# A two-layer conditioned block with Strassen products: a start on quarters of Wq and Wk, three more two-level products in one layer, x^T added by GpSimd, and a rewritten output stage

## The chip, the cores and the metric

One core of a Trainium2 chip runs the whole program. The metric is the device time of one execution in microseconds (us); the kernel before takes 1194.61 us, the median of three runs (1192.78 to 1195.8).

## The reference, cut to what matters

Four batches of 512 tokens and 512 features go through two stages, all in float32. In the code V is 512, HID is 2048.

```
q, k, v  = x @ Wq, x @ Wk, x @ Wv
attn_out = softmax(q @ k^T * 512**-0.5) @ v @ Wp + bp
cms      = gelu(attn_out @ cW1 + cb1) @ cW2 + cb2 + one_hot(code)
modifier = gelu(concat(attn_out, cms) @ mW1 + mb1) @ mW2 + mb2
y        = clip(x + cms + modifier, 0, 1)
# second stage; W_down (512x256), W_up (256x512), b_*, ln_* are picked
# for each batch out of three by an index
h        = gelu(y @ W_down[e] + b_down[e]) @ W_up[e] + b_up[e] + y
out      = (h - mean(h)) * rsqrt(var(h) + 1e-5) * ln_w[e] + ln_b[e]
```

Every output of every row is computed from all of these; the large products are those with cW1, cW2, mW1 and mW2.

## The kernel before, in words

**Products.** The kernel holds activations feature-first (features on the 128 partitions, tokens along the free dimension) and works on two batches (a pair) at a time, so a block of 1024 tokens is halved into its two batches. The large products are done with the seven products of Strassen's scheme (in Winograd's form) in place of eight, numbered 1 to 7 in the code: 1 = a11 b11, 2 = a12 b21, 3 = s4 b22, 4 = a22 t4, and 5, 6, 7 = s1 t1, s2 t2, s3 t3. Sums of weights (s) are formed by GpSimd (`weight_sums`, L178 to L181), sums of activations (t) by VectorE (`token_sums`, L190). A product is called one-level when each of its blocks is multiplied plainly, and two-level when the block is once more split into seven.

**Stages, in order.** (1) The fold: Wq^T and Wk^T are turned on TensorE with a multiplication by the identity (`transposed`, L416), their blocks and sums are evacuated from PSUM (`left_from_psum`, `right_from_psum`, L681 and L641), and `folded` multiplies Wq*Wk^T in seven products of `small_product` (L659). Then x of batch 0 and 1 is turned (L416 again). (2) Attention for pair 0 and pair 1 (L595, L659). (3) For each pair four layers: `c1_layer` (cW1; one-level products at L1065, two-level at L1014), `second_layer` for cW2 (L1215), `m1_layer` for mW1 (L1131, all products two-level), `second_layer` for mW2 (L1215). (4) For each batch an adapter: `load_adapter` gathers the weights by indirect DMA (L1286), and `adapter` turns y (`res_ps`, L1314), adds b_up on GpSimd (L1318), multiplies by W_down (L1323) and W_up (L1335), adds the turned y (L1343) and normalises (L1345 to L1369). The adapters of pair 0 run inside `c1_layer` of pair 1, step by step; those of pair 1 close the kernel.

**In `c1_layer`** products 1 and 5 of cW1 are two-level (`c1_two_level`), and 2, 6, 7, 3 and 4 one-level. The order is `FIRST_C = (2, 1, 5, 6, 7, 3, 4)`. Sums of cW1 for the two-level products (`c1_inner`) are made once by GpSimd in stage 2, stored to DRAM and fetched by both pairs.

**Who orders what.** Weights come through four buffers `wslot` of 1 MB, taken in turn; their fetches stand on the SP queue (`nc.sync`), so a fetch is issued when the product that used its buffer is done. GpSimd does the expansions of weights as a list of steps (`expansion()` for cW1, cW2 and mW1 in stages 2 and 3, `late_expansion()` for mW2 beside `m1_layer` of pair 0), and its queue also issues the stores of these sums. Its instructions stand in one order with those DMAs. Some VectorE instructions are pinned in program order (`keep_in_program_order`); the rest are placed by a scheduler. PSUM has eight banks, used in turn.

**Buffers that matter below.** `slot` 0 to 7 are 1 MB buffers (`wide` is slots 0 and 1). `late_expansion` loads raw weights into slots 6 and 7, which `second_operands` of the next layer writes with VectorE (L190), pinned. `mod` is scratch in `c1_layer` and the result of mW2 after it. After `m1_layer`, two DMAs with an adding write (L1419) put x^T onto `cms`.

Of the kernel before, what the change touches and what calls it, by code (L numbers as in the profile page):

```python
# [8 lines left out]
F32 = mybir.dt.float32  # L9
# [9 lines left out]
def kernel(  # L19
# [103 lines left out]
    wq = weight((nc.sync, nc.scalar, nc.sync, nc.scalar), Wq, slot[0])  # L123
    wk = weight((nc.sync, nc.scalar, nc.sync, nc.scalar), Wk, slot[1])
# [12 lines left out]
    x_rows = [load_x(0, nc.scalar, x_places[0])]  # L137
    wv = weight((nc.scalar, nc.scalar), Wv, slot[2])
    x_rows.append(load_x(1, nc.sync, x_places[1]))
# [34 lines left out]


# [19 lines left out]
    def flat(t):  # L195
# [3 lines left out]

    c1_outer = [spill.tile([P, 3, 2, 2, 256], F32, name=f"c1_outer{u}") for u in range(2)]  # L200
    c1_inner = {
        (p, u): spill.tile([P, n], F32, name=f"c1_inner_{p}_{u}")
        for p, n in ((1, 1024), (5, 2048))
# [13 lines left out]
    def expand_c1(u, then):  # L217
# [23 lines left out]
        yield  # L241

# [43 lines left out]
    def expand(unit, raw, pairs, last, then):  # L286
# [46 lines left out]
        else:  # L333
# [3 lines left out]
            yield from plain((1, a11, two), (4, a22, one))  # L337
            yield from full((5, one), (7, three), (6, two))
            then()

    def expand_all(units, raw, pairs, last):
        if last is None:
            load_raw(*units[0][:2], units[0][3], raw)
        for n, unit in enumerate(units):

            def then():
                if n + 1 < len(units):
                    load_raw(*units[n + 1][:2], units[n + 1][3], raw)

            yield from expand(unit, raw, pairs, last, then)  # L350
# [19 lines left out]
    def late_expansion():  # L370

        yield from expand_all(m2_units, slot[6:8], (flat(mod[0]), flat(mod[1]), slot[0]), None)
# [38 lines left out]
    def transposed(get, dst, finish=None):  # L411

        ps = [bank("tr_ps") for d in range(4)]
# [5 lines left out]
        for d in range(4):  # L419
            if finish is None:  # L420
                evacuate(dst[:, d, :], ps[d])
            else:
                finish(d, ps[d])
# [228 lines left out]
    def small_product(lhs, rhs, keep, then=None, copy=nc.scalar.copy):  # L652


        def matmuls(p, _, ps, first_):
# [14 lines left out]
            (1, 5, 6, 2, 7, 3, 4), then, copy,  # L670
# [5 lines left out]
    def left_from_psum(t, s):  # L676

        s1, s2, s3, s4 = (s[:, k] for k in range(4))

        def finish(d, ps):  # L680
            nc.scalar.copy(t[:, d, :], ps)  # L681
            c = d % 2
            if d < 2:
                minus(s3[:, c], ps[:, :256], t[:, c, 256:])
            else:
                minus(s2[:, c], ps[:, 256:], s3[:, c])
                add(s1[:, c], ps[:, 256:], t[:, c, 256:])
                minus(s4[:, c], ps[:, :256], s2[:, c])

        return finish  # L690

    def folded(lhs, rhs, w, s):
# [17 lines left out]
        small_product(lhs, rhs, keep)  # L710
# [71 lines left out]
    def first_operand(pair):  # L782
        xT, t_x = places(pair)
        transposed(chunks(x_rows[2 * pair]), xT[0], right_from_psum(xT[0], sums_in(flat(t_x[0]))))
# [17 lines left out]
    transposed(chunks(wq), wq_t, left_from_psum(wq_t, s_q))  # L802
    transposed(chunks(wk), wk_t, right_from_psum(wk_t, t_k))
    lhs_qk = folded(left_operand(wq_t, s_q), right_operand(wk_t, t_k), w_qk, sums_in(slot[0]))
    first_operand(0)
    load_bias()
    begun = both_operands(0)
    for pair in range(B // 2):
# [59 lines left out]
        if pair == 0:  # L868
            begun = {}
            then = {6: [lambda: first_operand(1)], 4: [lambda: begun.update(both_operands(1))]}  # L870
# [89 lines left out]
    def c1_operands(slots=(0, 1, 2, 3)):  # L960

        at0, at1, t12, t34 = (in_rows[i] for i in slots)
        b11, b12, b21, b22 = at0[:, 0:2, :], at1[:, 0:2, :], at0[:, 2:4, :], at1[:, 2:4, :]
        t1, t2, t3, t4 = t12[:, 0:2, :], t12[:, 2:4, :], t34[:, 0:2, :], t34[:, 2:4, :]

        def inner_sums(k, t):
            s = mod[1][:, 2 * k : 2 * k + 2, :].rearrange("p a (b n) -> p (a b) n", b=2)
            return inner_operands(t, 1, [s[:, i : i + 1, :] for i in range(4)], pinned=True)
# [4 lines left out]
        one = {1: inner_sums(0, b11)}  # L973
        minus(t1, b12, b11)

        def rest():
            one[5] = inner_sums(1, t1)
# [6 lines left out]
        return one, {2: b21, 3: b22, 4: t4, 6: t2, 7: t3}, rest()  # L984
# [531 lines left out]
```

## Time and profile before

| | us |
|---|---|
| three runs: median (lowest to highest) | 1194.61 (1192.78 to 1195.8) |
| the profiled execution, its device time | 1194.26 |
| its span, first to last instruction | 1192.5 |
| TensorE (matmul) busy | 1168.9 |
| VectorE / ScalarE / GpSimd busy | 883.5 / 294.9 / 482.7 |
| TensorE's first instruction, last end | 4.39, about 1181.1 |

The device time is 1.76 us above the span, and the profiled execution is 0.35 us below the median. A float32 matmul stands in the trace as two passes, each with a weight load (PEld); a turn by the identity is one pass. "128x512" is partitions by elements. In the views, the number in brackets is the idle time of the engine ahead of the line, with what ended it. The duration of one matmul (379 or 592 ns) includes its latency; what a pass costs in a row of matmuls is read from the distance of their starts. Idle time of TensorE sums to 23.6 us (1192.5 - 1168.9).

### The profile page before, as it was taken

The page shows a single profiled execution, that of the slowest core. Times are in us where ns is not written, and L with a number is a line of the kernel's source. Part 1 is how long each engine was busy: PE and PEld are TensorE (multiplying, and loading weights), DVE is VectorE, ACT ScalarE, POOL GpSimd, SP SyncE. Part 2 cuts the span into 40 slices and gives each one's busy share as a digit, 9 for nine tenths or more (in the row PEclk, how much of TensorE's full clock was granted, in tenths as well). Part 3 has the DMA queues.
Part 4 walks back from the last instruction along what each step waited for, and adds up shares of the span by engine and source line. Part 5 has one row for each costly group of instructions (what it writes and reads, how often), then busy time and mean ns, then how long its engine had stood idle before and what let it go on. Part 6 is the DMA issues. An engine that isn't in the chain of part 4 may idle for free.

```text
span 1192.5 us, 13167 instructions
## 1 busy us (share of the span) xinstructions
PE 1168.9 (98%) x4809; PEld 894.8 (75%) x4809; DVE 883.5 (74%) x1221; ACT 294.9 (25%) x540; POOL 482.7 (40%) x542
## 2 busy tenths in 40 slices
PE   7999999999999999999999999999999999999996
PEld 6478558747468888888888857447888888888872
DVE  4735565476789867897899837779894588699947
ACT  3234325335520000012310037551000002220014
POOL 4788999988940048870000522110000010124015
PEclk9999999999999999999999999999999999999998
DMA  8743695698756478787737553132735454775601
GB/s 289 277 149 135 245 351 196 218 389 331 262 194 249 176 279 319 283 293 251 241 134 297 177 177 133 54 132 106 293 131 187 166 211 168 219 240 187 228 1 71
DMA packets 78368, 251.50 MB, mean 211 GB/s; under 512 B 7348, under 2 KB 34016, under 8 KB 63456
## 3 DMA queue, kind: packets, MB, share of 16 engines
q1 hardware_dynamic: 54768, 149.96, 35.0%
q0 software_dynamic: 20736, 89.17, 21.2%
q10 hardware_dynamic: 2800, 11.54, 2.5%
q8 instruction: 38, 0.62, 0.2%
q14 instruction: 26, 0.21, 0.1%
HBM read 185.63 MB, written 65.01 MB: 210 GB/s over the span
## 4 chain that ended last, share of the span: by engine, by line
PE 92%; DMA 3%; DVE 2%; POOL 2%; ACT 1%; SPq 1%; issue 0%; ACTq 0%; DVEq 0%; POOLq 0%
PE i L1215 28%; PE i L1131 27%; PE c L1065 10%; PE sum L595 8%; PE sum L659 7%; PE sum L1014 4%; PE down_ps L1323 2%; PE up_ps L1335 2%; DMA wslot<-c_inner 1%; DMA wslot<-in_L_cond_mW 1%; PE tr_ps L416 1%; PE prod_ps L430 1%; PE res_ps L1314 1%; DMA wide<-in_L_cond_Wk 1%; SPq L988 1%
## 5 line engine op out<-in xcount | busy, mean ns | idle before, releaser
L1131 PE MATMUL i<-slot,wslot 128*128 128x256 f32 x1184 | 260.8, 379 | 0.0
L1131 PEld LDWEIGHTS i<-slot,wslot 128*128 128x128 f32 x1184 | 225.0, 190 | 30.6
L1215 PE MATMUL i<-slot,wslot 128*128 128x256 f32 x896 | 202.5, 379 | 0.0
L1215 PEld LDWEIGHTS i<-slot,wslot 128*128 128x128 f32 x896 | 170.2, 190 | 23.1
L906 ACT COPY first<-i 128x256 f32<-128x256 f32 (+1 forms) x56 | 26.8, 479 | 544.9 <-PE i L1215 280.6
L1215 PE MATMUL i<-hidden,wslot 128*128 128x256 f32 x576 | 132.2, 379 | 0.0
L899 DVE TENSOR_TENSOR part<-i,part 128x512 f32<-128x512 f32 (+1 forms) x156 | 90.9, 591 | 43.1 <-PE i L1131 26.6
L1215 PEld LDWEIGHTS i<-hidden,wslot 128*128 128x128 f32 x576 | 109.4, 190 | 16.2 <-issue 1.4
L928 ACT ACTIVATE hidden<-hidden,bias 128x512 f32<-128x512 f32 x128 | 85.2, 716 | 61.8 <-DVE hidden L505 60.7
L1065 PE MATMUL c<-slot,wslot 128*128 128x512 f32 x224 | 97.3, 592 | 0.0
L1065 PEld LDWEIGHTS c<-slot,wslot 128*128 128x128 f32 x224 | 42.5, 190 | 53.1 <-issue 50.5
L1286 POOL DMA_INDIRECT slot<-in_L_cond_W_down,idx_d x12 | 15.5, 1288 | 149.8 <-PE i L1215 88.2
L1286 POOL DMA_INDIRECT slot<-in_L_cond_b_up,idx_e x3 | 4.3, 1420 | 174.1 <-PE i L1131 173.5
L505 DVE TENSOR_TENSOR sum<-sum,wslot 128x512 f32<-128x512 f32 x51 | 35.4, 697 | 36.8 <-PE sum L659 18.7
L190 DVE TENSOR_TENSOR slot<-hidden,slot 128x1024 f32<-128x1024 f32 x48 | 58.4, 1217 | 0.3
L190 DVE TENSOR_TENSOR slot<-hidden 128x1024 f32<-128x1024 f32 x48 | 58.4, 1216 | 0.0
L899 DVE TENSOR_TENSOR part<-i,first 128x512 f32<-128x512 f32 (+1 forms) x62 | 36.3, 589 | 28.6 <-PE i L1131 16.2
L505 DVE TENSOR_TENSOR hidden<-c,hidden 128x512 f32<-128x512 f32 x64 | 43.3, 688 | 15.5 <-PE c L1065 14.3
L659 PE MATMUL sum<-hidden,wslot 128*128 128x256 f32 x232 | 53.5, 380 | 0.4 <-POOL wslot L180 0.4
L284 POOL DMA_DIRECT2D slot<-in_L_cond_mW x24 | 17.9, 753 | 81.4 <-DVE slot L190 80.5
L659 PEld LDWEIGHTS sum<-hidden,wslot 128*128 128x128 f32 x232 | 43.6, 190 | 6.8 <-POOL wslot L180 0.8
L505 DVE TENSOR_TENSOR hidden<-part,hidden 128x2048 f32<-128x2048 f32 x20 | 48.1, 2405 | 0.5
(307 smaller groups left out, 1988.6 us busy)
## 6 DMA issues: line engine op xcount, KB each, us to landing
wslot<-m_kept SPq DMA_DIRECT2D x48, 1024.0 KB
wslot<-m_kept SPq DMA_DIRECT2D x36, 512.0 KB
wslot<-c_kept SPq DMA_DIRECT2D x16, 1024.0 KB
slot<-in_L_cond_mW POOLq DMA_DIRECT2D x24, 512.0 KB
wslot<-in_L_cond_mW SPq DMA_DIRECT2D x24, 512.0 KB
slot<-in_L_cond_cW POOLq DMA_DIRECT2D x16, 512.0 KB
wslot<-in_L_cond_cW SPq DMA_DIRECT2D x32, 256.0 KB
m_kept<-wide POOLq DMA_DIRECT2D x6, 1024.0 KB
```

The costliest lines, as they stand in the source:

```text
L190: i = eng.tensor_tensor(out_, one, two, ALU.subtract)
L505: nc.vector.tensor_tensor(dst, a, b, ALU.add)
L595: nc.tensor.matmul(ps, lhsT=lhs[p][:, c, r * P : (r + 1) * P], rhs=rhs[p][:, c, :], start=(first_ and c == 0), stop=(c == 1), skip_group_c ...
L659: nc.tensor.matmul(v[:, j, :], lhsT=lhs[p][:, c, j * P : (j + 1) * P], rhs=rhs[p][:, c, :], start=(first_ and j == 0 and c == 0), stop=(c ...
L899: nc.vector.tensor_tensor(dst, ps, other, ALU.add)
L906: nc.scalar.copy(c1, p1)
L928: nc.scalar.activation(block[:, t, :], block[:, t, :], AF.Gelu, bias=bias_c[:, 8 * half + t : 8 * half + t + 1],)
L1014: nc.tensor.matmul(halves_of(ps)[:, j, :], lhsT=a[g][:, at_[q], j * P : (j + 1) * P], rhs=rhs[q][:, 0, :], start=(first_ and j == 0), stop ...
L1065: nc.tensor.matmul(ps, lhsT=lhs(c, t), rhs=one_level[p][:, c, :], start=(c == 0), stop=(c == 1),)
L1131: nc.tensor.matmul(out_ps[:, j, :], lhsT=a[j][q][:, c, :], rhs=now[q][:, c, :], start=(c == 0), stop=(c == 1),)
L1215: nc.tensor.matmul(ps[:, :256], lhsT=a[k // 2][q][:, k % 2, :], rhs=now[q][:, k, :], start=(k == 0), stop=(k == 3),)
L1323: nc.tensor.matmul(ps, lhsT=wd[:, c, n * P : (n + 1) * P], rhs=y[:, c, :], start=(c == 0), stop=(c == NV - 1),)
```

## The change

1. *Start.* Wq comes as four quarters (256 rows by 256 columns) on the SP queue, Wk likewise on the ScalarE queue; x of batches 0 and 1, Wv and Wp follow on the SP queue. Each pair of quarters is turned as it lands; product 1 of the fold is issued after the first pair. The products go in the order 1, 2, 5, 6, 7, 3, 4, and x of batch 0 is turned between 6 and 7. Ahead of it all, TensorE multiplies 15 times a 128x128 tile of zeros, and ScalarE copies one column (`touched`) at once.
2. *cW1.* For pair 1, products 2, 6 and 7 are two-level too. `late_expansion` gets six more steps on GpSimd that load blocks of cW1 or its stored sums, form four sums each, and store them. In those products' `keep`, and for their activation sums, GpSimd does adds (`h22 + h21`, `inner_sums`).
3. *First difference of the second layer.* Except in `c1_layer` of pair 0, `t1 = h12 - h11` (lower half) is made by a ScalarE copy with scale -1 and an adding DMA from the GpSimd queue, in place of VectorE.
4. *x^T.* A plain DMA loads it to slot 3 and four GpSimd adds (128x512) put it onto `cms`, for each batch.
5. *Adapters.* b_up is added feature-first by ScalarE (`with_bias`); y is turned into the same PSUM bank in which the W_up product accumulates, and the statistics are read from PSUM. GpSimd is left one add for most tiles, none for the last of a batch; in the last batch the last two tiles end on VectorE. In the last batch W_down is done in halves of 256 tokens, and two output tiles stand ahead of its last quarter.

```
+    QUARTERS = ((0, 0), (0, 1), (1, 0), (1, 1))
+    wq = quarters(Wq, slot[0], nc.sync)
+    wk = quarters(Wk, slot[1], nc.scalar)
...
+    x_rows = [load_x(b, nc.sync, x_places[b]) for b in range(2)]
+    wv = weight((nc.sync, nc.sync), Wv, slot[2])
...
+    nc.scalar.copy(touched, eps)
+    zeros = const.tile([P, P], F32, name="zeros")
+    nc.vector.memset(zeros, 0.0)
+    idle_ps = bank("idle_ps")
+    for _ in range(15):
+        nc.tensor.matmul(idle_ps[:, :P], lhsT=zeros, rhs=zeros, start=True, stop=True)
...
+    both_quarters(0, 0)
+    lhs_qk = folded(
+        lhs_q, rhs_k, w_qk, sums_in(slot[0]),
+        {
+            1: [lambda r=r, k=k: both_quarters(r, k) for r, k in QUARTERS[1:]],
+            6: [lambda: ends.append(first_operand(0))],
+            7: [lambda: ends[0]()],
+        },
+    )
...
-        for p, n in ((1, 1024), (5, 2048))
+        for p, n in ((1, 1024), (5, 2048), (2, 1024), (6, 1024), (7, 1024))
...
+    def expand_c1_late(raws, sums):
+        units = [(p, u) for p in (2, 6, 7) for u in range(2)]
...
+        def rest():
+            for i, (p, u) in enumerate(units):
+                raw = block_of(i)
+                to = sums[i % 4].rearrange("p (k n) -> p k n", k=4)
+                weight_sums(
+                    raw[:, 0, 0], raw[:, 0, 1], raw[:, 1, 0], raw[:, 1, 1],
+                    *(to[:, k] for k in range(4)),
+                )
+                if i + 4 < len(units):
+                    load(i + 4)
+                nc.gpsimd.dma_start(out=c1_inner[p, u], in_=sums[i % 4])
+                yield
...
+            else:
+                add(h21, z, h21)
+                nc.gpsimd.tensor_tensor({6: h12, 7: h22}[p], h22, h21, ALU.add)
...
+        two = [p for p in FIRST_C if p in ((2, 1, 5, 6, 7) if more else (1, 5))]
...
+            if (p, g) == (3, 0) and not busy:
+                for two in (slice(0, 2), slice(2, 4)):
+                    tc.keep_in_program_order(
+                        nc.scalar.activation(t1[:, two, :], h11[:, two, :], AF.Copy, scale=-1.0)
+                    )
...
+                    nc.gpsimd.dma_start(out=t1[:, LOW, :], in_=h12[:, LOW, :], accum_op=ALU.add)
...
+        def with_input(s, pair=pair):
+            tc.keep_in_program_order(nc.gpsimd.dma_start(out=in_rows[3], in_=xT_kept[2 * pair + s]))
+            for d in range(4):
+                tc.keep_in_program_order(
+                    nc.gpsimd.tensor_tensor(
+                        cms[s][:, d, :], cms[s][:, d, :], in_rows[3][:, d, :], ALU.add
+                    )
+                )
...
-            nc.gpsimd.dma_start(out=cms[s], in_=xT_kept[2 * pair + s], accum_op=ALU.add)
...
+    def up(g, wu, y1, aff, h, t):
+        ps = bank("up_ps")
+        for c in range(NV):
+            nc.tensor.matmul(
+                ps[:, c * P : (c + 1) * P], lhsT=y1[:, c, t * P : (t + 1) * P], rhs=ident,
+                is_transpose=True, start=(c == 0), stop=True, skip_group_check=True,
+            )
+        for n in range(NB):
+            nc.tensor.matmul(
+                ps,
...
+        nc.vector.bn_stats(stats, ps)
...
+        nc.vector.scalar_tensor_tensor(h, ps, mv[:, 0:1], aff[:, 0, :], ALU.subtract, ALU.mult)
...
+        if t == NT - 1 or last and t == NT - 2:
+            nc.vector.scalar_tensor_tensor(h, h, rstd, aff[:, 1, :], ALU.mult, ALU.add)
+        else:
+            nc.scalar.activation(h, h, AF.Copy, scale=rstd)
+            nc.gpsimd.tensor_tensor(h, h, aff[:, 1, :], ALU.add)
...
+    def last_adapter(b, y, loaded, g, rows, y1, eng):
+        wd, wu, bd, bu, aff = loaded
+        with_bias(y, bu, y1)
+        first_half, second_half = slice(0, 256), slice(256, 512)
+        for n, tokens in ((0, first_half), (1, first_half), (0, second_half)):
+            down(y, wd, bd, g, n, tokens)
+        mvs = [up(g, wu, y1, aff, rows[:, t, :], t) for t in range(2)]
+        down(y, wd, bd, g, 1, second_half)
+        for t in range(NT):
+            if t > 1:
+                mvs.append(up(g, wu, y1, aff, rows[:, t, :], t))
+            normalised(b, rows[:, t, :], mvs[t], aff, t, eng, last=True)
```

## The prediction

> **What bounds the kernel now.** I read the busy times first, then TensorE's timeline for every idle stretch, then the chain of work that ended last.
>
> ```profile
> PE 1168.9 (98%) x4809; PEld 894.8 (75%) x4809; DVE 883.5 (74%) x1221; ACT 294.9 (25%) x540; POOL 482.7 (40%) x542
> ```
>
> TensorE is the bound: 23.6 us of the span of 1192.5 are its idle time. A gain must come out of these 23.6 us or shorten TensorE's own work; time saved on another engine counts only where TensorE waits for it. TensorE's timeline puts the idle time in three places. The start:
>
> ```profile
> 4.39 3.64 PE L416 MATMUL tr_ps<-ident,wide 128*128 128x128 f32 x16 [4.39 <-DMA wide<-in_L_cond_Wq]
> 8.20 2.92 PE L416 MATMUL tr_ps<-ident,wide 128*128 128x128 f32 x16 [0.16 <-DMA wide<-in_L_cond_Wk]
> 12.71 2.05 PE L659 MATMUL sum<-hidden 128*128 128x256 f32 x8 [1.59 <-ACT hidden L641]
> ```
>
> The reader is to see 6.1 us of waiting ahead of the first product, and turns that are slow: 16 in 3.64 us, where 16 later turns take 1.91.
>
> The middle, the largest of six small waits there:
>
> ```profile
> 541.85 1.13 PE L1131 MATMUL i<-cms,wslot 128*128 128x256 f32 x4 [1.35 <-DMA wslot<-in_L_cond_mW]
> ```
>
> Together these are about 6 us; this one, in `m1_layer` of pair 0, comes while GpSimd's stores of expanded weights fill the DMA engines (414 GB/s from 540 to 545).
>
> The end, in the chain of waits and then on the SP queue:
>
> ```profile
> 1187.29 0.69 DVE hidden L1368
> ```
>
> ```profile
> 1188.01 0.33 SPq L1369 DMA_DIRECT2D out<-hidden  x1
> ```
>
> TensorE is done at 1181.12, VectorE finishes the last two output tiles, and the last store is issued 7.2 us after TensorE's end; 4.2 us more pass until the span ends.
>
> **What the Trainium skill says.** "TensorE: Matmul & The Clock Gate", Part 1 (the HAM clock gate): TensorE starts at half clock and goes to full after a busy window of about 3.4 us whose phase is free. The trace agrees: 228 ns for one turn at first, 119 ns later, full speed from about 9.5 us, some 5 us after the first turn. "ScalarE: Activation LUTs", What ACT_TABLE_LOAD costs: 1283 ns to switch sets; here 1.28 us at 8.82, and it stands on the path. "DMA: Bandwidth & Descriptors", Queues, rings and completion order: DMA engines go round the queues packet by packet, so GpSimd's transfers slow SP's fetches; the wait at 541.85 is such a case (2 MB fetched in 15 us).
>
> **The change, part by part.**
>
> *Three two-level products.* From starts in `c1_layer` of pair 1: 16 passes of 128x512 take 6.87 us (742.71 to 749.58), or 429 ns each; 16 passes of 128x256 take 3.45 us (712.17 to 715.62), 216 ns each. One one-level product is 32 passes: 13.73 us. A two-level one is 7 x 2 x 2 matmuls, 56 passes: 12.08 us. Three of them take off 3 x 1.65 = 4.95 us, all on the path. The cover: per product 6 or 7, VectorE does 16 adds of 0.69 us = 11.0 against 12.1 us of TensorE plus the adapter steps between them (6 to 10 us), and the adapters lose an add, a scale and a shift per tile on VectorE. GpSimd does 8 adds of 1.27 = 10.2 us in the same time, and PSUM's eight banks come round in time if VectorE keeps up. Without that cover the cost is one to two microseconds a product. One wait of 0.87 us in this stage (for VectorE) may stay or go; I count it as staying. Value -4.95, from -5.8 to -2.
>
> *The start.* Removed: the first 4.39 us, the table load on the path (`touched` takes it to the start), and the 1.59 us for the evacuation. Added: the zeros. VectorE's first memset is at 0.80, so TensorE starts at about 1.1 us with 30 passes of 228 ns, 6.8 us if the clock stays low throughout, fewer once it rises. With the rise 3.4 to 6.8 us after the start the zeros end between 6.2 and 7.9 us; I take 7.0. The first pair of quarters is there before that (the first quarter of Wq was there at 4.39; 2 MB were moved by 8.0 in the windows of 1 us, so the last by about 8.5 to 9). Then: 8 turns 0.95, evacuation 0.7 (ScalarE 0.58 plus the hand-over), product 1 of 8 passes 1.72, 24 turns 2.8, six products 10.35 with x's turn 1.9, the biases 0.26 and the second x 1.9: TensorE reaches the first attention product at 7.0 + 20.6 = 27.6 us, against 28.79. Value -1.2, from -2.0 to -0.3. VectorE's six differences of 0.69 us behind the last quarter lie beside products 2, 5 and 6. GpSimd's chain, for which TensorE waits 0.38 at 117.34, begins with the landing of x of batch 0 (16.54); x now comes right behind Wq, so that moves forward too and does not hold the gain back.
>
> *The end.* TensorE's work there is equal: 16 turns move from ahead of W_down to W_up, and 16 matmuls of 128x256 in place of 8 of 128x512 cost 6.90 against 6.87. After TensorE's end E, with two tiles left: VectorE does the third from E - 2.0 (one tile is 2.2 us of TensorE) in 0.69 + 0.18 + 0.7 + 0.15 + 0.98 = 2.7, then the fourth in the same 2.7, so at E + 3.4; with 0.35 to issue, 3.75 us in place of 7.2. The adds and scalings on GpSimd and the six VectorE operations that stood behind one another there are gone. Value -3.3, from -4.0 to -2.0 (the scalar_tensor_tensor took 0.98 to 1.56 us here when GpSimd worked beside it). The number of table loads is the same.
>
> *GpSimd's six more steps.* 24 adds of 0.72 us, six stores of 0.56 and eight loads: 17 + 3 + 5 = 25 us of GpSimd and 6 MB of DMA, about 16 us at 385 GB/s. GpSimd is idle from 533.2 to 551.9, but the DMA engines are not: up to 545 they run full. SP's fetches of mW1 stand against 6 MB more. Queued behind on GpSimd are only x^T and later gathers, needed some 30 us later. Value +1.0 (0 to +4).
>
> *x^T and the first difference.* Two loads and eight adds of 1.27 us on GpSimd in place of two adding DMAs: nothing waits for them before the mW2 layer adds to y, over 30 us on. The difference takes 2.3 us off VectorE where TensorE doesn't wait for it; the adding DMA has a whole product (24 us) before it is read. Both 0; if the DMA came late, the third product of the second layer would wait, at most some 3 us.
>
> Sum: -1.2 - 4.95 - 3.3 + 1.0 = -8.45. The profiled execution of 1194.26 becomes 1185.8. The median of the runs is 0.35 higher: 1186.2.
>
> **Rivals.**
>
> *The covers hold better than I take them* (1182 to 1183.5): zeros end at 6.2 (-0.8), the wait of 0.87 goes, no new DMA wait (-1.0), and the 1.35 goes with an earlier fetch: 1186.2 - 0.8 - 0.9 - 1.0 - 0.7 = 1182.8. For it: VectorE has 57 us of work in 91 us of that stage now. Against: late in mW1 the DMA engines are already full.
>
> *The gain is eaten in `c1_layer` or by the fetches* (1189 to 1193). If VectorE or the banks cost 1.5 us for each of products 2, 6 and 7, 4.5 of 4.95 us are lost, giving 1190.7. Against: the two two-level products that are there now lose 0.87 in all.
>
> *Slower:* GpSimd's late steps hold slots 6 and 7. VectorE writes them, pinned, for the mW2 layer (L190, from 592.57), and TensorE waits for that. I have GpSimd done at about 562. If each of the six steps takes a DMA round trip, 12 us (GpSimd waited 6.3, 4.7 and 3.5 us for such loads), they end at 533 + 72 = 605, 13 us late, and 13 - 9.45 = +3.6 gives 1198.2. The break-even is an end at about 601. Against: four loads are issued ahead, so the trips overlap.
>
> *It does not do what it says:* the zeros could keep TensorE from the first quarter for longer than they save, which costs the 1.2 us alone (1187.4) and lies in the main case.
>
> **How the numbers follow.** Main case 0.62 (1183.5 to 1189), better covers 0.13, eaten gain 0.18, slower 0.05, rest 0.02 about level. 0.3% is 3.6 us, about what a measurement of this kernel can tell from no change: faster is below 1191.0. Of the eaten gain two thirds lies below that: 0.62 + 0.13 + 0.12 = 0.87 faster, 0.08 within, 0.05 slower. The range takes in the better cover and the eaten gain up to 1191: 1182.3 to 1191.
>
> **What would show it.** Right: TensorE's first attention product at about 27.6 us; `c1_layer` of pair 1 shorter by 5 us with no wait over 1 us in it; the last store issued 3.5 to 4.5 us after TensorE's end; waits for mW fetches between 500 and 570 of about 2.4 us in sum. Wrong: turns still at 228 ns after the zeros; waits for VectorE or GpSimd at the two-level products; GpSimd busy with late sums after 590; a first matmul of the mW2 layer that waits for VectorE.

## The result and the profile after

The changed kernel takes 1184.26 us (median of four runs, 1182.89 to 1184.47) against 1193.69 us for the kernel before, run beside it (four runs, 1192.54 to 1195.8). The ratio is 0.9922, with a 95% interval of 0.9901 to 0.9943: faster, and by more than 0.3%. Forecast were 1186.2 us and a range of 1182.3 to 1191.0.

The profiled execution of the changed kernel is the fastest of its four (1182.89 us, span 1181.1), so it stands 11.4 us below that of before where the medians differ by 9.4. By the busy times TensorE is still the bound, with 14.7 us idle where it had 23.6:

```profile
PE 1166.4 (99%) x4927; PEld 914.7 (77%) x4927; DVE 879.3 (74%) x1187; ACT 295.0 (25%) x536; POOL 568.8 (48%) x629
```

Cut TensorE's timeline at the first matmul of each stage, and the 11.4 us fall apart as follows (us; "end" is from TensorE's last end to the end of the span):

| stage | before | after | change | forecast |
|---|---|---|---|---|
| start, to the first attention product | 28.79 | 27.66 | -1.13 | -1.2 |
| attention, both pairs | 222.17 | 220.12 | -2.05 | 0 |
| cW1, pair 0 | 95.13 | 94.43 | -0.70 | 0 |
| mW1, pair 0 | 170.82 | 171.75 | +0.93 | +1.0 |
| cW1, pair 1 | 125.25 | 118.88 | -6.37 | -4.95 |
| mW1, pair 1 | 169.22 | 169.68 | +0.46 | 0 |
| mW2 of pair 1 and adapters | 115.92 | 115.78 | -0.14 | 0 |
| end | 11.38 | 8.98 | -2.40 | -3.3 |

The layers with cW2 and mW2 that are not listed took 84.6 us each in both.

*The start.* TensorE's timeline, with start and duration in us and the idle time in brackets:

```profile
1.08 6.21 PE L193 MATMUL idle_ps<-zeros 128*128 128x128 f32 x30 [1.08 <-DVE zeros L190]
7.13 1.04 PE L875 MATMUL tr_ps<-ident,wide 128*128 128x128 f32 x8
9.04 1.97 PE L739 MATMUL sum<-hidden 128*128 128x256 f32 x8 [0.88 <-DVE hidden L888]
...
27.66 3.60 PE L673 MATMUL sum<-hidden,cms 128*128 128x512 f32 x8
```

The zeros end at 7.1 us, the first 8 turns take 1.04 us, and one wait of 0.88 us for the evacuation is left. Counted from start to start, a turn stands 109 ns behind the one before it, where the passes over the zeros stood 213 ns apart until 6.6 us; 109 is called full speed below.

*cW1 of pair 1.* In the kernel before, TensorE lost 1.44 us in this stage, counted from the starts of its matmuls: 1.13 at a wait for VectorE, 0.06 just ahead of it, and 0.25 in the first W_up product, in gaps too short for a bracket. TensorE's timeline there:

```profile
708.48 2.13 PE L1335 MATMUL up_ps<-slot,first 128*128 128x512 f32 x4
...
732.93 1.03 PE L1014 MATMUL sum<-mod,wslot 128*128 128x256 f32 x4
734.82 1.13 PE L1014 MATMUL sum<-mod,wslot 128*128 128x256 f32 x4 [0.87 <-DVE sum L505]
```

In the changed kernel the stage begins at 683.18. These are its last groups and the first of the next layer; no line of the stage has a bracket, and the starts show no lost time:

```profile
770.28 7.03 PE L1214 MATMUL c<-wide,wslot 128*128 128x512 f32 x16
...
788.33 13.90 PE L1214 MATMUL c<-slot,wslot 128*128 128x512 f32 x32
802.06 1.89 PE L1380 MATMUL i<-hidden,wslot 128*128 128x256 f32 x8
```

*Attention.* Two waits of the kernel before are gone, one for VectorE and one for GpSimd. With the short gaps around them they cost 1.15 and 0.88 us:

```profile
43.57 3.70 PE L595 MATMUL sum<-mod,wide 128*128 128x512 f32 x8 [0.88 <-DVE sum L505]
...
117.34 3.96 PE L659 MATMUL sum<-hidden,wslot 128*128 128x256 f32 x16 [0.38 <-POOL wslot L180]
```

*mW1 of pair 0.* The wait of 1.35 us for a fetch is gone, and another of nearly the same size has come, for VectorE:

```profile
506.01 1.97 PE L1282 MATMUL i<-slot,wslot 128*128 128x256 f32 x8 [1.33 <-DVE part L1009]
```

VectorE's own timeline tells why it was late. The first of two adds of the same size took 6.60 us; such an add takes 2.28 us when nothing disturbs it:

```profile
488.18 6.60 DVE L583 TENSOR_TENSOR hidden<-part,hidden 128x2048 f32<-128x2048 f32 x1
494.81 2.70 DVE L583 TENSOR_TENSOR hidden<-hidden,hidden 128x2048 f32<-128x2048 f32 x1
```

*The end.* TensorE is done at 1172.12. The timeline of the other engines:

```profile
1170.96 2.49 POOL L1531 TENSOR_TENSOR hidden<-hidden,wide 128x512 f32<-128x512 f32 x2 [12.61 <-ACT hidden L1530]
...
1172.44 1.56 DVE L1528 SCALAR_TENSOR_TENSOR hidden<-hidden,rstd,wide 128x512 f32<-128x512 f32 x1
1173.92 0.69 DVE L1514 BATCH_NORM_STATS2 stats<-up_ps 128x6 f32<-128x512 f32 x1
...
1175.72 0.75 DVE L1528 SCALAR_TENSOR_TENSOR hidden<-hidden,rstd,wide 128x512 f32<-128x512 f32 x1
```

VectorE's last result is there 4.35 us after TensorE's end (6.86 before; 3.4 forecast). The third tile's last instruction, at 1172.44, stands beside GpSimd's two adds and takes 1.56 us, twice the 0.75 of the fourth tile's.

### The profile page after: what moved, and what is told of

Same layout as the page of the kernel before. It is cut to its first block, busy times and chain, and to the rows that moved or that the text cites. A ratio compares the mean times of both kernels' runs of the same rounds, so it can differ in the third digit from the quotient of the medians.

```text
span 1181.1 us, 13509 instructions
## 1 busy us (share of the span) xinstructions
PE 1166.4 (99%) x4927; PEld 914.7 (77%) x4927; DVE 879.3 (74%) x1187; ACT 295.0 (25%) x536; POOL 568.8 (48%) x629
## 3 DMA queue, kind: packets, MB, share of 16 engines
q0 software_dynamic: 23120, 97.57, 23.5%
## 4 chain that ended last, share of the span: by engine, by line
PE 92%; DMA 3%; DVE 2%; ACT 1%; SPq 1%; issue 0%
PE i L1380 29%; PE i L1282 25%; PE sum L739 8%; PE sum L673 8%; PE c L1214 7%; PE sum L1139 7%; PE down_ps L1486 2%; DMA wslot<-in_L_cond_mW 2%; PE up_ps L1505 2%; PE tr_ps L490 1%; DMA wslot<-c_inner 1%; PE prod_ps L508 1%; DVE hidden L583 1%; DVE slot L210 1%; PE idle_ps L193 1%; PE up_ps L1500 1%
## 5 line engine op out<-in xcount | busy, mean ns | idle before, releaser
L1605 POOL DMA_DIRECT2D slot<-xT_kept x4 | 2.9, 715 | 165.2 <-PE i L1282 165.2
L1214 PE MATMUL c<-slot,wslot 128*128 128x512 f32 x160 | 69.2, 592 | 0.0
L210 DVE TENSOR_TENSOR slot<-hidden 128x1024 f32<-128x1024 f32 x48 | 61.5, 1282 | 0.0
L1608 POOL TENSOR_TENSOR cms<-cms,slot 128x512 f32<-128x512 f32 x16 | 27.1, 1714 | 71.6 <-PE i L1282 51.0
L1214 PEld LDWEIGHTS c<-slot,wslot 128*128 128x128 f32 x160 | 30.4, 190 | 38.3 <-issue 34.9
L583 DVE TENSOR_TENSOR hidden<-part,hidden 128x2048 f32<-128x2048 f32 x20 | 55.0, 2751 | 0.5
L1139 PE MATMUL sum<-mod,wslot 128*128 128x256 f32 x224 | 52.0, 379 | 0.2 <-DMA wslot<-c_inner 0.2
L1139 PEld LDWEIGHTS sum<-mod,wslot 128*128 128x128 f32 x224 | 42.5, 190 | 6.3 <-ACT mod L648 0.5
```

What stands on the lines that cost most here:

```text
L210: i = eng.tensor_tensor(out_, one, two, ALU.subtract)
L583: nc.vector.tensor_tensor(dst, a, b, ALU.add)
L1139: nc.tensor.matmul(halves_of(ps)[:, j, :], lhsT=a[g][:, at_[q], j * P : (j + 1) * P], rhs=rhs[q][:, 0, :], start=(first_ and j == 0), stop ...
L1214: nc.tensor.matmul(ps, lhsT=lhs(c, t), rhs=operands[p][:, c, :], start=(c == 0), stop=(c == 1),)
L1608: nc.gpsimd.tensor_tensor(cms[s][:, d, :], cms[s][:, d, :], in_rows[3][:, d, :], ALU.add)
```

## The experiments

The theory that the experiments test: each stage's change belongs to the part of the edit that touches it, and waits of TensorE that differ elsewhere (in attention, and in cW1 and mW1 of pair 0) come from the order and time in which VectorE, GpSimd and DMA meet. The rivals: the gain in cW1 comes from waits and adapters and not from fewer passes; the zeros only delay; the new wait in mW1 is caused by GpSimd's six steps.

The table has the times of all twelve runs, in the order of the sections below, and the stages of the one execution of each that was profiled (us, read from TensorE's timeline as above; "p0" and "p1" are the two pairs, "last" is VectorE's last result behind TensorE's end). All are compared with the kernel before on the same chip.

| run | median (runs) | ratio, 95% interval | first product | attention | cW1 p0 | mW1 p0 | cW1 p1 | mW1 p1 | last |
|---|---|---|---|---|---|---|---|---|---|
| no_zeros | 1183.12 (4) | 0.9923 (0.9895 to 0.9951) | 28.92 | 220.13 | 95.78 | 169.22 | 118.88 | 169.21 | 4.34 |
| one_level | 1190.03 (15) | 0.9972 (0.9960 to 0.9984) | 27.69 | 220.14 | 95.53 | 172.84 | 124.18 | 169.21 | 4.34 |
| old_start | 1184.24 (4) | 0.9918 (0.9894 to 0.9942) | 27.93 | 221.44 | 95.51 | 171.97 | 118.88 | 169.21 | 4.35 |
| tail_order | 1181.31 (4) | 0.9895 (0.9873 to 0.9918) | 27.09 | 221.14 | 97.27 | 171.98 | 118.88 | 169.47 | 2.91 |
| then_late | 1189.80 (20) | 0.9964 (0.9946 to 0.9982) | 27.45 | 221.93 | 97.06 | 175.90 | 118.88 | 169.61 | 4.35 |
| plain_c1 | 1190.29 (19) | 0.9974 (0.9960 to 0.9988) | 27.27 | 220.37 | 96.10 | 169.51 | 124.30 | 169.21 | 4.34 |
| zeros_8 | 1186.26 (15) | 0.9945 (0.9930 to 0.9961) | 26.06 | 223.55 | 95.34 | 169.80 | 118.88 | 169.58 | 4.35 |
| x_by_dma | 1193.86 (12) | 1.0009 (0.9984 to 1.0035) | 27.40 | 220.35 | 97.65 | 176.00 | 118.88 | 173.67 | 4.34 |
| both_undone | 1182.39 (4) | 0.9918 (0.9896 to 0.9941) | 26.76 | 221.87 | 94.56 | 170.55 | 118.88 | 169.21 | 4.35 |
| t1_vector | 1182.77 (4) | 0.9911 (0.9888 to 0.9934) | 27.27 | 220.47 | 97.09 | 169.28 | 118.88 | 169.21 | 4.34 |
| best | 1183.18 (6) | 0.9924 (0.9906 to 0.9943) | 27.56 | 220.76 | 95.25 | 171.59 | 118.88 | 169.21 | 2.92 |
| changed_again | 1183.58 (6) | 0.9924 (0.9904 to 0.9944) | 27.27 | 221.20 | 95.64 | 169.69 | 118.88 | 169.67 | 4.34 |

A single time of the kernel before lay anywhere from 1188.97 to 1199.58 us in these comparisons, so a stage of a trace tells what a median can't.

### Without the zeros

```
-    for _ in range(15):
+    for _ in range(0):
```

> The changed kernel without the fifteen multiplications of zeros; all else as it is. Theory (the zeros pay by warming TensorE): the first 8 turns take 228 ns each, the pause of some 0.9 us for the evacuation puts the rise of the clock off to about 12 us, product 1 and most of the 24 next turns run at half speed, and the first attention product starts at 29 to 30 us, against 27.66 with the zeros: slower by 1.5 to 2.5 us. Rival (the zeros only stand in the way): the first turn starts at about 4.5 us, when the first quarters have landed, the clock rises about 5.2 us later all the same, and the first attention product starts at about 27.0 us, 0.7 us earlier than with the zeros. Everything behind the first attention product as in the changed kernel.

The first product started at 28.92 us, 1.26 us later than with the zeros. That is the theory by direction, and less than the 1.5 to 2.5 us expected. TensorE's timeline:

```profile
4.51 1.94 PE L875 MATMUL tr_ps<-ident,wide 128*128 128x128 f32 x8 [4.51 <-DMA wide<-in_L_cond_Wq]
7.33 3.75 PE L739 MATMUL sum<-hidden 128*128 128x256 f32 x8 [0.87 <-DVE hidden L888]
10.87 4.02 PE L875 MATMUL tr_ps<-ident,wide 128*128 128x128 f32 x24
```

Product 1 takes 3.54 us to the next group's start in place of 1.80, and the 24 turns 3.86 in place of 2.62. By their starts, 12 of the 24 turns were still slow (213 ns), so full speed came at 13.4 us, 8.9 us after the first turn. With the zeros it came at 6.6 us, 5.5 us after TensorE's first instruction. That the pause of 0.87 us put the rise off is likely, but one profile does not show it. The median is no higher than with the zeros: 1.3 us is below what these medians tell apart.

### Products 2, 6 and 7 one-level again

```
-        two = [p for p in FIRST_C if p in ((2, 1, 5, 6, 7) if more else (1, 5))]
+        two = [p for p in FIRST_C if p in (1, 5)]
...
-        yield from rest
```

> The changed kernel with products 2, 6 and 7 of cW1 one-level again in pair 1, and without the six late GpSimd steps that make their sums. Theory (32 passes against 56 halves, 1.65 us a product): the stage of cW1 in pair 1, 118.9 us now, becomes 123.8 us plus at most the 0.87 us wait for VectorE that the kernel before had; the stage of mW1 in pair 0, 171.75 us now, falls to about 170.8 as before, since GpSimd's six steps are gone; median 1184.3 + 4.95 - 0.95 = 1188.3. Rival (the gain of 6.4 us in that stage came mostly from the rewritten adapters and from waits): the stage stays within 2 us of 118.9 and the median at 1184 to 1186. Rival on GpSimd (the wait of 1.33 us for VectorE in mW1 has nothing to do with the six steps): the wait of over 1 us stays in that stage.

The stage of cW1 went to 124.18 us, 5.30 more, without a bracketed wait. By the starts, 0.36 us of it is short gaps of TensorE, which leaves 4.94 for the passes, as forecast (4.95). The expectation for mW1 of pair 0 failed. Without GpSimd's six steps the stage was no shorter but 1.1 us longer, with three waits for VectorE. VectorE's and GpSimd's timelines there:

```profile
489.32 11.69 DVE L582 TENSOR_TENSOR hidden<-part,hidden 128x2048 f32<-128x2048 f32 x1
501.05 2.69 DVE L582 TENSOR_TENSOR hidden<-hidden,hidden 128x2048 f32<-128x2048 f32 x1
```

```profile
490.89 2.34 POOL L362 TENSOR_TENSOR wide<-slot 128x1024 f32<-128x1024 f32 x1
493.20 0.71 POOL L199 TENSOR_TENSOR mod<-mod,slot 128x256 f32<-128x256 f32 x1
...
496.49 2.36 POOL L362 TENSOR_TENSOR slot<-slot,mod 128x1024 f32<-128x1024 f32 x1
498.80 2.79 POOL L200 TENSOR_TENSOR mod<-mod 128x256 f32<-128x256 f32 x1
```

One add of VectorE stood for 11.69 us, while GpSimd went through its queue without slowing down (0.71 us for 128x256, 2.34 for 128x1024); then GpSimd was the one that stood (2.79 us for what takes 0.71). The times fit: 9.41 us are left of the 11.69 when 2.28 for the add itself are taken off, and GpSimd's slow instruction begins 9.48 us after VectorE's add. The Trainium skill, "SBUF — State Buffer", Who interferes with whom, says that a VectorE instruction with two SBUF inputs contends with a GpSimd instruction that reads SBUF, and calls the shared ports an exclusive lock. The traces agree, and go further: VectorE was held over a run of seven GpSimd instructions, not over one.

### The start of the kernel before

```
-    wq = quarters(Wq, slot[0], nc.sync)
-    wk = quarters(Wk, slot[1], nc.scalar)
+    wq = weight((nc.sync, nc.scalar, nc.sync, nc.scalar), Wq, slot[0])
+    wk = weight((nc.sync, nc.scalar, nc.sync, nc.scalar), Wk, slot[1])
...
-    for _ in range(15):
-        nc.tensor.matmul(idle_ps[:, :P], lhsT=zeros, rhs=zeros, start=True, stop=True)
...
+    transposed(chunks(wq), wq_t, left_from_psum(wq_t, s_q))
+    transposed(chunks(wk), wk_t, right_from_psum(wk_t, t_k))
```

> The changed kernel with the start of the kernel before: no zeros, whole Wq and Wk in halves on two queues, x loaded later, the fold in its old order. Theory (the start alone took away TensorE's waits in the attention of the two pairs, because x and the work of VectorE and GpSimd come earlier): first attention product at 28.8 us, and the waits of 0.88 us for VectorE near 43.6 and 0.38 for GpSimd near 117 are back, so that the attention stage ends 1.1 + 2.0 us later than in the changed kernel; median 1184.3 + 3 = 1187.3. Rival (those waits come and go from run to run, or left for another reason): only the 1.1 us of the start come back and no wait for VectorE near 43.6; median 1185.4.

The wait for VectorE in attention is back, to the hundredth:

```profile
42.72 3.70 PE L653 MATMUL sum<-mod,wide 128*128 128x512 f32 x8 [0.88 <-DVE sum L563]
```

The wait for GpSimd near 117 is not back, and attention took 1.3 us more than in the changed kernel, so half of the theory stands. The first product came at 27.93 us, earlier than the 28.8 expected, since the turns reached full speed sooner in this run (32 in 6.09 us). The median, 1184.24, says nothing on 1.3 us.

### Only one tile ahead of the last quarter of W_down

```
-        mvs = [up(g, wu, y1, aff, rows[:, t, :], t) for t in range(2)]
+        mvs = [up(g, wu, y1, aff, rows[:, 0, :], 0)]
         down(y, wd, bd, g, 1, second_half)
         for t in range(NT):
-            if t > 1:
+            if t > 0:
```

> The changed kernel with one edit in the last adapter: the last quarter of W_down stands after one output tile in place of two, so that its gelu, the table load for the square root and GpSimd's two adds come 2.2 us earlier. Theory (the end is 1 us longer than forecast because the final scalar_tensor_tensor of the third tile, 1.56 us beside GpSimd's adds, takes twice its 0.75): that instruction takes 0.75 us, the last store is issued about 3.7 us after TensorE's end in place of 4.5, and the time falls by 0.8 us. Rival (VectorE would be late anyway, or TensorE waits for the gelu of the last quarter with only one tile to cover it): the third tile's scalar_tensor_tensor stays near 1.5 us or a new wait of TensorE of 0.5 us or more appears near the end, and the time stays.

The timeline of the end, with TensorE done at 1175.43:

```profile
1173.78 1.27 POOL L1531 TENSOR_TENSOR hidden<-hidden,wide 128x512 f32<-128x512 f32 x1 [0.39 <-ACT hidden L1530]
1175.12 0.75 DVE L1528 SCALAR_TENSOR_TENSOR hidden<-hidden,rstd,wide 128x512 f32<-128x512 f32 x1
...
1177.59 0.75 DVE L1528 SCALAR_TENSOR_TENSOR hidden<-hidden,rstd,wide 128x512 f32<-128x512 f32 x1
```

GpSimd is done before VectorE's instruction begins, which now takes 0.75 us. The last result is there 2.91 us after TensorE's end, 1.44 sooner, and TensorE has no new wait at the end. The theory holds, with more than the 0.8 us expected, because VectorE no longer waits for the square root of the third tile either.

### GpSimd's raw loads issued late, as before

One line of the change, which neither its description nor the prediction names, moves the loads of the next raw weights ahead of the last three steps of a unit. This run puts it back. (A second such line lets GpSimd take three steps in place of two at each turn of `m1_layer`; no run undoes it.)

```
             yield from plain((1, a11, two), (4, a22, one))
-            then()
             yield from full((5, one), (7, three), (6, two))
+            then()
```

> The changed kernel with one line of its GpSimd expansion put back: the loads of the next raw weights are issued behind the last three steps of a unit, not ahead of them. Theory (the earlier loads take away GpSimd's pauses for DMA, so that its adds run without a break and lock VectorE's adds of 128x2048 out, 6.6 us in place of 2.3, and TensorE waits 1.3 us for VectorE in the mW1 stage of pair 0): the long add takes under 4.5 us, no wait for VectorE of over 0.5 us is left in that stage, a wait of about 1 us for a fetch of mW1 may come back, and the stage goes from 171.75 us to between 169.2 and 170.8; the time falls by 1 to 2 us or stays. Rival (the lockout comes from the chance at which instruction VectorE and GpSimd meet, not from the loads): the stage stays at 171.5 to 172.5 with a wait for VectorE of 1 us or more.

The long add took 3.30 us and the wait for VectorE was gone. That does not show the theory, because the changed kernel's second profile (below) has an add of 3.48 us and no such wait either. The stage went to 175.90 us, 4.2 more, and the time to 1189.80, in one long wait for a fetch:

```profile
545.79 2.08 PE L1282 MATMUL i<-cms,wslot 128*128 128x256 f32 x4 [4.93 <-DMA wslot<-in_L_cond_mW]
```

```profile
571.42 0.56 POOL L302 DMA_DIRECT2D c_inner<-mod  x1 [0.30 <-POOL mod L201]
```

GpSimd's last store stands at 571.42, against 555.66 in the changed kernel. Six of the eight loads are now issued from 533 to 538 us, right behind the stores of mW2's sums, while a fetch issued at 527.9 is under way; it lands only at 545.7. The theory of the wait stays open, and it misses the price of its edit; the earlier loads are what makes the six steps cheap.

### cW1 of pair 1 as in pair 0

```
-        for _ in c1_layer(h, c1_rhs, made[2], final, lambda: steps(extra, 1)):
-            if not final:
-                steps(between, 2)
+        for _ in c1_layer(h, c1_rhs, made[2], False, None):
+            steps(between, 2)
...
-        yield from rest
```

> The changed kernel with cW1 of pair 1 done just as in pair 0 and as in the kernel before: products 2, 6 and 7 one-level, the sums of activations by VectorE, no late steps of GpSimd. Only the rewritten adapters are left of the change in that stage, which took 125.25 us before, 118.88 in the changed kernel and 124.18 with one-level products but sums by GpSimd. Theory (the two-level products give 4.95 us, the rewritten adapters, which lose work on VectorE, the other 1.1 us with the wait of 0.87): 124.0 to 124.3 us and no wait of over 0.5 us. Rival (the wait went because GpSimd forms the sums of activations): 125.0 to 125.5 us with a wait for VectorE of about 0.9 us.

124.30 us, with one small wait:

```profile
712.51 1.99 PE L1138 MATMUL sum<-mod,wslot 128*128 128x256 f32 x8 [0.21 <-DVE sum L582]
```

By the starts, TensorE loses 0.48 us around this wait, so of the 5.42 us that this run gives back, 4.94 are the passes, the same as in the run with one-level products. The other 1.43 of the 6.37 us are lost time that went: 0.95 with the rewritten adapters alone, whose wait for VectorE shrank from 0.87 to 0.21, and the last 0.48 only in the whole change. mW1 of pair 0 took 169.51, again without the six steps, where one_level had 172.84: that stage's waits don't follow the steps.

### Eight zeros

```
-    for _ in range(15):
+    for _ in range(8):
```

> The changed kernel with 8 multiplications of zeros in place of 15. Theory (the clock rises some 5 us after TensorE's first instruction as long as it has work, and the first quarters land at about 4.5 us): the zeros end at about 4.8 us, the first turns start there, at half speed until about 6.3 us, product 1 starts at about 7.4 us at full speed, and the first attention product at 26.0 us in place of 27.66. Rival (the turns alone, with the pause of 0.9 us for the evacuation, do not carry the rise): product 1 at half speed, 3.7 us, and the first attention product at 27.5 to 28.5 us. Rival (the next quarters have not landed): a wait for DMA ahead of the 24 turns and no gain over 0.5 us.

The first product started at 26.06, as expected, 1.6 us sooner. It did not last: attention took 3.4 us more, and the median is 1186.26 us. TensorE's timeline, and GpSimd's in this run, in the changed kernel and in the run without zeros:

```profile
115.96 3.99 PE L739 MATMUL sum<-hidden,wslot 128*128 128x256 f32 x16 [1.65 <-POOL wslot L200]
```

```profile
101.60 2.37 POOL L362 TENSOR_TENSOR wide<-slot 128x1024 f32<-128x1024 f32 x1
103.94 1.27 POOL L198 TENSOR_TENSOR wslot<-hidden 128x512 f32<-128x512 f32 x1
```

```profile
99.92 1.28 POOL L198 TENSOR_TENSOR wslot<-hidden 128x512 f32<-128x512 f32 x1
101.16 2.37 POOL L362 TENSOR_TENSOR wide<-slot 128x1024 f32<-128x1024 f32 x1
```

```profile
97.34 2.37 POOL L362 TENSOR_TENSOR wide<-slot 128x1024 f32<-128x1024 f32 x1
99.66 1.28 POOL L198 TENSOR_TENSOR wslot<-hidden 128x512 f32<-128x512 f32 x1
```

An edit at 5 us has changed GpSimd's order at 100 us: a 2.37 us step of an expansion now stands ahead of the sums that TensorE waits for. The order alone does not cost the 3.4 us, though. The run without zeros has the same order of GpSimd's instructions up to 120 us, and no wait for GpSimd in attention (220.13 us). There GpSimd came to this step 4.3 us earlier (its four longest waits up to then sum to 22.8 us, here to 27.1), and TensorE's first product came 2.9 us later. Why GpSimd was later here is open.

### x^T by an adding DMA

```
-            tc.keep_in_program_order(nc.gpsimd.dma_start(out=in_rows[3], in_=xT_kept[2 * pair + s]))
-            for d in range(4):
-                tc.keep_in_program_order(
-                    nc.gpsimd.tensor_tensor(
-                        cms[s][:, d, :], cms[s][:, d, :], in_rows[3][:, d, :], ALU.add
-                    )
-                )
+            tc.keep_in_program_order(
+                nc.gpsimd.dma_start(out=cms[s], in_=xT_kept[2 * pair + s], accum_op=ALU.add)
+            )
```

> The changed kernel with x^T put on by two adding DMAs, as before, in place of a load and four GpSimd adds. Theory (this part costs and gives nothing): the same stage times within 0.5 us and the same median, 1184.3, within 1.5 us. Rival (GpSimd's adds and the extra load are what delays a fetch of mW1 by 0.4 us late in that stage of pair 0, and 0.2 us and more beside VectorE in pair 1): the wait of 0.39 us near 586 is gone and the mW1 stage of pair 1 takes 169.2 in place of 169.7, 0.9 us less in all.

Neither theory nor rival held: the time is 1193.86 us, no faster than the kernel before. mW1 is 4.25 us longer in pair 0 and 3.99 in pair 1, in waits for fetches such as this one:

```profile
591.61 1.10 PE L1282 MATMUL i<-slot,wslot 128*128 128x256 f32 x4 [2.68 <-DMA wslot<-in_L_cond_mW]
```

The DMA view of 572 to 589 us, by queue (packets, MB, share of the engines' time) and by transfer (the last number is us from issue to landing):

```profile
q0 software_dynamic: 287, 2.10, 67.7%
q1 hardware_dynamic: 1159, 1.90, 32.1%
...
wide<-hidden POOLq DMA_DIRECT2D x1, 1024.0 KB, 8.6
...
cms<-xT_kept POOLq DMA_DIRECT2D x1, 1024.0 KB, 14.4
wslot<-in_L_cond_mW SPq DMA_DIRECT2D x2, 512.0 KB, 15.6
```

The two adding DMAs of 1 MB (the first difference and x^T) took 67.7% of 17 us of all engines, 5.5 us a MB, where the fetches took 2.9 us a MB. It is not GpSimd's queue as such that is dear: over the whole span of the changed kernel it moved 97.57 MB in 23.5% of the engines' time, 2.8 us a MB. The fetch behind the two landed after 15.6 us, and a product lasts 12.1.

### Both adding-DMA edits undone, and one of them

x_by_dma's edit and, in second_operands, `busy = True` for all layers (the first difference by VectorE):

> The changed kernel with x^T put on by adding DMAs and the first difference of the second layer formed by VectorE, both as in the kernel before. Theory (with x^T by adding DMA the changed kernel lost about 4 us in the mW1 stage of each pair, because the adding DMA of the first difference and that of x^T then stand on the DMA engines together, within 3 us of each other, and hold up the fetches of mW1; either of them alone does little): the waits of 2.5 us for fetches of mW1 late in that stage are gone, the stage takes 169.2 to 169.8 us in pair 1 and up to 172 in pair 0, and the median is within 2 us of the changed kernel, 1183 to 1186. Rival (the two adding DMAs of x^T alone, beside GpSimd's 6 MB more, are what costs): the waits stay in pair 0 and the median is 1188 or more.

The time is 1182.39 us and mW1 of pair 1 takes 169.21 us, with x^T by adding DMA as in x_by_dma: the theory holds. The changed kernel has the other adding DMA alone and is as fast, so it is the two together that cost x_by_dma some 9 us. With `busy = True` alone:

> The changed kernel with only the first difference of the second layer formed by VectorE, as before, and x^T still by a load and GpSimd's adds. Theory (VectorE has room late in the mW1 stage and in cW1 of pair 1, and one adding DMA less stands on the DMA engines): the wait of some 0.4 us for a fetch of mW1 near 586 us goes, the mW1 stage of pair 1 takes 169.2 in place of 169.7, cW1 of pair 1 stays at 118.9, median 1184 or 0.5 us less. Rival (VectorE's 2.3 us stand ahead of the adds that free PSUM): a wait for VectorE of 0.5 to 2 us near the end of the first layers, cW1 of pair 1 at 119.5 to 121, and 1 to 4 us more in all.

mW1 of pair 0 and 1 took 169.28 and 169.21 and cW1 of pair 1 118.88; three waits for VectorE of 0.3 to 0.4 us stand in the mW2 layer of pair 0, which took 86.48 us. The median, 1182.77, is the changed kernel's within the spread.

### A version from the findings

both_undone with tail_order's edit, beside the changed kernel itself:

> The changed kernel with three edits: x^T by adding DMAs and the first difference by VectorE, both as in the kernel before, and the last quarter of W_down behind one output tile in place of two. Theory (the end's gain stands by itself): the span ends 7.3 us after TensorE's last end in place of 9.0, the mW1 stage of pair 1 takes 169.2 us, and the median lies 1.5 to 2.5 us below that of the changed kernel on the same chip, at 1181 to 1182.5. Rival (the difference drowns in the waits for GpSimd and DMA in attention and in cW1 and mW1 of pair 0, which move by some 3 us from run to run): median within 1 us of the changed kernel's.

> The changed kernel itself, beside the version above on the same chip, for the comparison of the two and for the spread of its stages: median 1183.5 to 1185; the cW1 stage of pair 1 at 118.9 us and the end at 9.0 us behind TensorE as before; the waits in attention, in cW1 of pair 0 and in mW1 of pair 0 may each differ by up to 2 us from the first profile if they come and go by chance, and by less than 0.3 us if they belong to the kernel.

The last result came 2.92 us after TensorE's end, against 4.34, but the medians are 1183.18 and 1183.58 with the same ratio of 0.9924: not told apart. The changed kernel's second profile has no wait for VectorE in mW1 of pair 0 (169.69 us in place of 171.75), one of 0.78 us for GpSimd in attention that the first had not, and 118.88 us for cW1 of pair 1 to the hundredth. The first two differ by chance; the last belongs to the kernel.

## Why the prediction was right, and where it was not

**The start** (-1.2; -1.13 measured): the terms are right, the zeros' end at 7.0 (7.1 measured) and the rest of the row of 20.6 us (20.5) included, but that the sum came so close is luck. In the ten profiles with fifteen zeros the first product started between 26.76 and 27.69 us, and with the old start at 28.79 and 27.93, so the gain is shown only as 0.2 to 2.0 us. What moves is the moment of full speed: 3.6 to 5.5 us after TensorE's first instruction in these ten, with unbroken work. The Trainium skill's busy window of about 3.4 us with free phase ("TensorE: Matmul & The Clock Gate", Part 1) agrees, if one takes from it the estimate of one to two windows, 3.4 to 6.8 us. The prediction read the speeds too slow: its 228 and 119 ns a turn contain the latency of the last one, from start to start they are 213 and 109, and full speed came at 10.2 us in the kernel before, not 9.5. The rival that the zeros cost the 1.2 fell: without them the first product came at 28.92. Fifteen are more than the start needs, though; with eight it came at 26.06.

**Three two-level products** (-4.95): the mechanism and the size are shown. Undoing them cost 5.30 and 5.42 us, of which 4.94 in both runs is passes and the rest new gaps. The cover held: no wait at all. The step that failed is "I count it as staying", of the wait of 0.87 us. It went, with all of the 1.44 us that TensorE lost in this stage before, and that is the 1.4 us by which the stage was under-forecast. The rewritten adapters alone, which lost work on VectorE, take away 0.95 of it in one profile; what takes the rest was not tested apart.

**The end** (-3.3, though 7.2 less 3.75 is 3.45; -2.40 in the span, -2.51 in VectorE's last result): the term for the third tile was mis-sized. It was put at 2.7 us with a scalar_tensor_tensor of 0.98; it took 3.95, from 1170.05 to 1174.00: 1.56 for that instruction beside GpSimd's adds, and some 0.6 of waiting for square roots, the second tile's and its own. tail_order takes both away. The fourth tile took 2.55 (2.7 forecast).

**GpSimd's six more steps** (+1.0; +0.93 in the stage): right by accident. The steps were taken to hold up fetches; the trace shows a wait for VectorE in their place, and it comes and goes with the run (169.69 in the second profile) and without the steps too (172.84 and 169.51). What the steps can cost through DMA, the run with GpSimd's loads issued late shows: 4 us, the upper end that was given, were it not for the loads moved ahead, a line that the prediction did not read. GpSimd was done at about 556, near the 562 forecast, and far from the 601 of the slower rival.

**x^T and the first difference** (0 and 0): right as a sum, wrong as two zeros. "Nothing waits for them" asked who waits for the data; the price is what the adding DMAs take from the fetches beside them. With x^T left on adding DMAs, the difference as an adding DMA took the whole gain (1193.86 us).

**Not forecast:** 2.05 us of attention. 1.15 of it is the wait of 0.88 us for VectorE with the short gaps around it, which belongs to the start's order (the run with the old start has it again). The rest is a wait for GpSimd, which is 0 in one profile of the changed kernel and 0.78 us in the other, and up to 1.51 in runs whose edits leave this stage alone. The DMA waits in cW1 of pair 0 differ in the same way (94.43 to 97.65 us over all runs). That the medians gave 9.4 us and the profiles 11.4 may lie in these; no run separates them further.

The reason for the forecast, TensorE's passes and idle time summed by stage, stood. The three gains came to -1.13, -6.37 and -2.40, or -9.9, near the -9.45 summed for them; that is in part luck, since cW1 gave 1.4 us more and the end 0.9 less. The profiled execution was forecast at 1185.8 us and took 1182.89, and most of that gap is the part of attention that was not forecast. (The waits in the middle of the kernel before, which the prediction counts as six, are eight in TensorE's timeline; their sum of about 6 us is right.)

## What to carry to other kernels

Ask of a transfer not only who waits for its data but what it takes from the transfers beside it: an adding DMA took twice the engine time per byte, and two of them within 3 us held up the fetches that the bound engine lives on. Read each stage's length in the trace against its passes; a stage that repeats to the hundredth is the kernel's, one that moves by 2 us between profiles is not to be credited to an edit. And a saving at the start can be lost 100 us later, where the bound engine, now early, meets another engine's queue in another order and at another time: look there before crediting it.

## What the runs showed of the hardware

A VectorE add with both inputs in SBUF took up to 11.69 us (2.28 alone) while GpSimd ran seven instructions in a row without slowing down, and afterwards GpSimd's next took 2.79 in place of 0.71. A scalar_tensor_tensor with both tensors in SBUF took 1.56 us beside a GpSimd add and 0.75 without; the one with its first input in PSUM took 0.73 to 0.75 either way. An adding DMA used 5.5 us of all 16 engines for a MB, a fetch beside it 2.9. TensorE began with passes of 128x128 that stood 213 ns apart and came to 109 ns 3.6 to 5.5 us after its first instruction with unbroken work (ten profiles of the same start), and after 8.9 us in the one profile where a pause of 0.87 us came between.
